# A two-layer vision tower on one core: moving preparation steps of the first attention to other chunks, and loading the second layer's weights and tokens during the expert attention

## The chip, the cores and the metric

The kernel runs on one core of a Trainium2 chip. The metric is the device time of one execution in microseconds (us); the time of a kernel is the median of its runs. A profile is one further execution, recorded by the hardware profiler, with an instruction-by-instruction trace.

## The reference

128 images of 128x128 pixels pass a convolutional tokenizer to 64 tokens of 256 features each. Two layers follow, each an attention and an "ffn", both with residual additions and a layer norm in front.

```
h = tokenizer(x)                                        # [128, 64, 256]
# layer 0
xn = layernorm(h); Q, K, V = xn @ Wq.T, xn @ Wk.T, xn @ Wv.T
attn[b,q,k,g] = relu(sum_d relu(Q[b,q,g,d] - K[b,k,g,d]) * w_mlp[d] + b_mlp)
h += softmax_k(attn) applied to V                       # 8 groups of 32 features
h = ffn0(layernorm(h))   # per 64-feature chunk: attention by 4 experts, gated, projected; plus residual
# layer 1
h += linear_attention(layernorm(h))  # softmax of q over features and of k over positions; k (x) v; times q
h += experts(layernorm(h))           # each token to one of 8 experts (capacity 1280), 256 -> 1024 -> 256
```

Everything is float32.

## The kernel before, in words

The stages run one after another: tokenizer; first attention (`relu_attention`); the ffn of layer 0 (`expert_attention`); the attention of layer 1 (`linear_attention`); routing and experts. Through the first three the activations stay on the chip in one tile `h2`, [128 partitions, 64 pairs of images, 256]; a partition holds one token of one of the two images of a pair. The order of the instructions is written out by hand: inside `tc.manual_schedule()` every engine executes its instructions in the order of the program.

**First attention.** Eight blocks of 16 images; each block is worked in eight chunks of eight query tokens, 64 chunks in all. A chunk needs, for 16 images and two halves of the features, the pairwise terms of queries and keys. They are made in three ways: `larger` (VectorE, a maximum, straight from the queries in PSUM), `difference` (GpSimd subtracts, ScalarE applies relu), and `by_query` (ScalarE alone, one token at a time). `add(i0, hf)` sums four images' terms over the features on TensorE. The eight additions of a chunk come in the order (0,0), (8,0), (4,0), (8,1), (0,1), (4,1), (12,0), (12,1); the first number is the first image, the second the half. Between them stand `queries` of the next chunk, `begin`, and the softmax of the chunk before: `less_max` on VectorE, `exponents` on ScalarE, `sums` on VectorE, `weights` on GpSimd, `transpose` on TensorE. The relu outputs pass through rings of buffers: `mg` has five, `ma` and `mv` three.

All that prepares the next block or finishes the last one is hung into the chunks by a table: `at(n, place, step)` puts a step into chunk n at a place. The places in the order of the program are O, X, A, V1, Y, B, W, Z, V2 and C; roughly, X, Y and Z are for TensorE, A, B, C and O for ScalarE, V1 and V2 for VectorE, W for GpSimd. With n = 8b for block b, `values(i)` (four pairs of projections of V) and their copies `valued(i)` are in chunks n-2, n-1 and n; `factors` (GpSimd: 1/sqrt(var) and the offset of the layer norm) at n-17 and n-13; `added(i)` (VectorE: outcome added to `h2`) in chunks n+10 to n+12. A chunk's number within its block of eight, n modulo 8, is called its position, or simply chunk 0 to chunk 7. Towards the end the places also hold the first steps of the expert attention (`beside`).

**Expert attention.** 64 pairs of images, one per turn of the loop in `rest`; each turn has the scores and softmax of pair p, the transposes, mixing and output of pair p-1 and the queries and values of pair p+1. `output` adds the result to `h2`, and every fourth pair a transfer on SP's queue stores four pairs to `hd`, a tensor in HBM.

**Linear attention.** It takes tokens in groups: a group is four token positions of all 128 images, so partition = image. `Group.load` brings a group from `hd`; `statistics` (VectorE), `factors` (GpSimd), `normal` (ScalarE) and `transpose` (TensorE, copied by ScalarE) prepare it. Four "heads" stages of 16 steps each then issue `queries_keys(i)`, while the table of this stage hangs in the rest. Before the first step come the loads of the weights on ScalarE's queue, of four groups on SP's queue, and the constants and the small loads of `Routing`.

SBUF tiles come from pools; a pool that opens where another was waits for the last use of that memory.

Of the kernel before, what the change touches and what calls it, by code (L numbers as in the profile page):

```python
# [290 lines left out]
class Shared:  # L291
# [3 lines left out]
    def __init__(self, c, ctx):  # L295
        def pool(name, bufs, **k):
            return ctx.enter_context(c.tc.tile_pool(name=name, bufs=bufs, **k))

        self.np_, self.bp = pool("an", 2), pool("ab", 2)
        self.atp, self.ep, self.small = pool("aat", 1), pool("ae", 2), pool("as", 1)  # L300
        self.psq = pool("apq", 4, space=PSUM)
# [5 lines left out]
def relu_attention(c, sh, wqkv, wmlp, bmlp, beside):  # L307
# [10 lines left out]
    with (  # L318
# [313 lines left out]
        for b, x in enumerate(blocks):  # L632
            n = 8 * b

            if b + 1 < len(blocks):
# [6 lines left out]
                for i in range(4):  # L642
                    at(n + 10 + i // 2, "XY"[i % 2], of(x.back, i))
                    at(n + 10 + (i + 1) // 2, ("V2", "V1")[i % 2], of(x.added, i))
# [15 lines left out]
            else:  # L660
                for i in range(NP):
                    at(n - 21 + i if b > 2 else 1 + i // 4, "V2", of(x.statistics, i))
                at(n - 17 if b > 2 else 2, "W", of(x.factors, 0, 4))
                at(n - 13, "W", of(x.factors, 4, 8))
# [16 lines left out]
            at(n - 2, "X", of(x.values, 0))  # L681
            at(n - 2, "A", of(x.valued, 0))
            at(n - 2, "Y", x.key_sums)
            at(n - 1, "V1", x.correction)
            at(n - 1, "X", of(x.values, 1))
            at(n - 1, "A", of(x.valued, 1))
            at(n - 1, "Z", of(x.values, 2))
            at(n, "O", of(x.valued, 2))
            at(n, "Y", of(x.values, 3))
            at(n, "B", of(x.valued, 3))  # L690
# [74 lines left out]
def expert_attention(c, sh, hd, normw, wr, br, wqkv, wvT, wproj, bproj, wout):  # L765
# [227 lines left out]
    class Pair:  # L993
# [89 lines left out]
        def weights(self, x):  # L1083

            e, sm = self.e[x], self.sm[x]
            s2 = sm.rearrange("p (m e) -> p m e", e=2)
            nc.gpsimd.tensor_mul(s2, s2, bcast(self.blk.gate[:, self.n, x::2], 1, 8))  # L1087
            nc.gpsimd.tensor_mul(e, e, bcast(sm, 2, T))  # L1088
# [31 lines left out]
        def output(self):  # L1120
# [5 lines left out]
            if p % 4 == 3:  # L1126
                nc.sync.dma_start(
                    hd[2 * p - 6 : 2 * p + 2].rearrange("(n b) t f -> (b t) n f", b=2),
                    h2[:, p - 3 : p + 1],
                )  # L1130

# [82 lines left out]
    def first(cur, new, chunk, last):  # L1214
# [39 lines left out]
        last.added(3)  # L1254
        for k in range(NB):
            x.stream(k)
# [3 lines left out]
    def rest(chunk, last):  # L1260
        with (
# [6 lines left out]
            for p in range(NP):  # L1268
                new = Pair(p + 1, blocks[(p + 1) // NB]) if p + 1 < NP else None
                if p == 0:  # L1270
                    first(cur, new, chunk, last)
                    old, cur = cur, new
                    continue
                do((p, "ACT"))
# [12 lines left out]
                cur.exponents(0)  # L1287
                if new:
# [8 lines left out]
                cur.weights(1)  # L1297
                do((p, "POOL"))
                old.mixed()
                if new:  # L1300
                    for h in range(2):
                        new.values(h)
                        new.values_kept(h)
                old.output()
# [11 lines left out]
def linear_attention(c, hd, hx, out, k, wqk, bqk, wv, bv, wgb):  # L1316
# [7 lines left out]
    NG = 4  # L1324
    with (
        tc.tile_pool(name="lw", bufs=1) as wp,
# [7 lines left out]
        w = wp.tile([P, 2, 2 * D], F32, name="w")  # L1334
        nc.scalar.dma_start(w, wqk.rearrange("(c p) n -> p c n", p=P))
        wvs = wp.tile([P, 2, D], F32, name="wvs")
        nc.scalar.dma_start(wvs, wv.rearrange("(c p) n -> p c n", p=P))
        bs = wp.tile([P, 2 * D], F32, name="bs")
        nc.scalar.dma_start(bs, bqk.partition_broadcast(P))
        bvs = wp.tile([P, 32], F32, name="bvs")  # L1340
        nc.scalar.dma_start(bvs, bv)

        wgs = wp.tile([P, 4, 32], F32, name="wgs")
        nc.gpsimd.memset(wgs, 0.0)
        for j in range(2):
            r = slice(j * 64, j * 64 + 64)
            nc.scalar.dma_start(wgs[r, :, j * E : j * E + E], wgb.rearrange("(p f) e -> f p e", f=64))
        ones = wp.tile([P, P], F32, name="ones")
        nc.gpsimd.memset(ones, 1.0)

        share = wp.tile([P, P], F32, name="share")
        nc.gpsimd.memset(share, 0.0)
        for hh in range(2):
            nc.gpsimd.memset(share[hh * 64 : hh * 64 + 64, hh * 64 : hh * 64 + 64], 1.0 / 64)

        class Group:
# [5 lines left out]
            def load(self):  # L1362
                g = self.g
                self.x = gp.tile([P, NG, D], F32, tag="x", name="x", bufs=4)
                nc.sync.dma_start(self.x, hd[:, g * NG : g * NG + NG, :])

            def statistics(self, j):
                if j == 0:
                    self.mv = gp.tile([P, NG, 2], F32, tag="mv", name="mv", bufs=4)
                    self.rs = gp.tile([P, NG], F32, tag="rs", name="rs", bufs=4)  # L1370
                    self.nb = gp.tile([P, NG], F32, tag="nb", name="nb", bufs=4)
                st = gp.tile([P, 6], F32, tag="st", name="st")
# [3 lines left out]
            def factors(self):  # L1376
                mean, var = self.mv[:, :, 0], self.mv[:, :, 1]
                nc.gpsimd.tensor_scalar_add(self.rs, var, LN_EPS)
                nc.gpsimd.tensor_tensor(self.rs, self.rs, c.nhalf[:, 0:NG], ALU.pow)
                nc.gpsimd.tensor_mul(self.nb, mean, self.rs)  # L1380
                nc.gpsimd.tensor_sub(self.nb, c.zero[:, 0:NG], self.nb)
# [250 lines left out]
        for n, x in enumerate(heads[:3]):  # L1632
# [35 lines left out]
            for k in range(2):  # L1668
                at(m + 1, 4 + 4 * k, x.gates, k)
                at(m + 1, 5 + 4 * k, x.gates_added, k)  # L1670

# [13 lines left out]
        def last():  # L1685
# [55 lines left out]
            t = gp.tile([P, NG, D], F32, tag="x", name="dev", bufs=4)  # L1741
            routing.statistics(t, gp.tile([P, NG, D], F32, tag="x", name="var", bufs=4))
# [22 lines left out]
        with tc.manual_schedule():  # L1765
            for g in range(4):
                groups[g].load()
            for g in range(3):
                for i in range(NG):
                    groups[g].statistics(i)  # L1770
                groups[g].factors()
                if g == 0:
                    for i in range(NG):
                        groups[0].normal(i)
                    groups[0].transpose()
            groups[4].load()
            for n, x in enumerate(heads):
# [15 lines left out]
class Routing:  # L1793


    def __init__(self, c, gp, wg, bg):
# [5 lines left out]
        self.bgs = gp.tile([P, E], F32, name="bgs")  # L1802
        nc.sync.dma_start(self.bgs, bg.partition_broadcast(P))
        wgs = gp.tile([P, 2, E], F32, name="wgs")
        nc.sync.dma_start(wgs, wg.rearrange("(c p) e -> p c e", p=P))
        self.ones = gp.tile([P, P], F32, name="ones")
        nc.gpsimd.memset(self.ones, 1.0)
        self.wsum = gp.tile([P, E], F32, name="wsum")
        with c.tc.tile_pool(name="gw", bufs=1, space=PSUM) as gpp:
            pw = gpp.tile([P, E], F32, name="pw")  # L1810
            for fc in range(2):
                nc.tensor.matmul(pw, self.ones, wgs[:, fc, :], start=(fc == 0), stop=(fc == 1))
            nc.vector.tensor_copy(self.wsum, pw)
# [13 lines left out]
        self.before = gp.tile([P, P], F32, name="before")  # L1827
# [4 lines left out]
        self.one = gp.tile([P, T], F32, name="one")  # L1832
        nc.vector.memset(self.one, 1.0)
        self.c = c
        self.mean, self.rs = (gp.tile([P, T], F32, name=n) for n in ("mean", "rs"))
# [329 lines left out]
def vit_tower(ctx: ExitStack, tc: tile.TileContext, a, out):  # L2165
# [8 lines left out]
    with tc.tile_pool(name="stream", bufs=1) as sp:  # L2174
        c.h2 = sp.tile([P, B // 2, D], F32, name="h2")
        tokenizer(c, a["x"], a["w1"], a["bn1"], a["w2"], a["bn2"])
        with ExitStack() as rings:
            sh = Shared(c, rings)
# [80 lines left out]
```

## Time and profile before

| | us |
|---|---|
| median of 3 runs (2669.07 to 2671.12) | 2670.72 |
| profiled execution, its own time | 2667.24 |
| its span, first to last instruction | 2665.5 |
| TensorE busy (share of the span) | 2523.5 (95%) |
| VectorE busy | 2009.8 (75%) |
| ScalarE busy | 1621.5 (61%) |
| GpSimd busy | 1627.9 (61%) |
| granted TensorE clock, mean | 0.983 |

Times inside the profile are microseconds from the span's start. PE is TensorE, PEld its weight loads, DVE VectorE, ACT ScalarE, POOL GpSimd, SP the engine whose queue issues most transfers. A line of the timeline or of the groups gives the engine, the line of the kernel (L340), the operation, "out<-in" by the program's names and, after "[", the idle time before it with what ended it. `x24` means that 24 instructions are merged. The chain of waits gives start, length and the instruction or transfer that everything after it waited for. A matmul's busy time counts pipelined instructions, so a busy TensorE may still wait inside.

The first attention runs from about 185 to 1060 us, with the additions as its largest row (L340), the expert attention until 1863.7, the linear attention until about 2160, routing until 2250 and the experts to the end.

### The profile page before, as it was taken

What the parts mean: (1) busy time and instruction counts of PE and PEld (TensorE: products, weight loads), DVE (VectorE), ACT (ScalarE), POOL (GpSimd) and SP (SyncE); (2) the same over time, 40 slices, a digit from 0 to 9 for tenths busy, and PEclk for the clock granted to TensorE, in tenths of its full rate; (3) what the DMA queues carried; (4) which work ended last, traced back from release to release, by engine and by line L of the source; (5) the groups of instructions that cost most, each with busy time, mean ns of one, the idle gap of its engine ahead of it and who ended that gap; (6) DMA issues with size and microseconds to landing.
All of it is one profiled execution on the core that took longest, in us unless ns stands there. A gap on an engine that the chain in (4) does not pass through costs nothing.

```text
span 2665.5 us, 81705 instructions
## 1 busy us (share of the span) xinstructions
PE 2523.5 (95%) x35613; PEld 1729.0 (65%) x35613; DVE 2009.8 (75%) x2998; ACT 1621.5 (61%) x3421; POOL 1627.9 (61%) x1426
## 2 busy tenths in 40 slices
PE   8989999999999999899999999998899987999997
PEld 4554444444444444688888888887466565888886
DVE  5759999999999999778787878776467786444443
ACT  2228889898898988666666666665344533232332
POOL 3319999999899999565666665643233313444544
PEclk9999999999999999999999999999899998999998
DMA  3000000000000000000000000000434454555554
GB/s 112 33 13 1 2 1 2 1 2 2 1 2 1 2 13 2 3 20 11 12 19 12 11 20 12 19 12 17 121 73 110 95 127 151 190 183 200 190 186 134
DMA packets 138274, 141.19 MB, mean 53 GB/s; under 512 B 107875, under 2 KB 121701, under 8 KB 130224
## 3 DMA queue, kind: packets, MB, share of 16 engines
q1 hardware_dynamic: 127536, 118.40, 14.7%
q0 software_dynamic: 7648, 14.77, 1.8%
q8 instruction: 281, 4.60, 0.7%
q10 hardware_dynamic: 2720, 2.69, 0.3%
q14 instruction: 89, 0.73, 0.1%
HBM read 104.03 MB, written 32.54 MB: 51 GB/s over the span
## 4 chain that ended last, share of the span: by engine, by line
PE 75%; DVE 13%; issue 5%; ACT 4%; POOL 2%; DMA 1%; SPq 0%; POOLq 0%; DVEq 0%; ACTq 0%
PE sc L340 15%; PE po L2103 6%; PE ph L2087 6%; PE pc L184 5%; PE pt L1097 4%; PE sc L1061 4%; PE pqk L1014 4%; PE pq L1421 4%; PE pv L1036 3%; PE pz L1110 3%; PE pt L587 2%; DVE m L530 2%; PE pc L459 2%; PE pk L405 2%; DVE mx L1073 2%
## 5 line engine op out<-in xcount | busy, mean ns | idle before, releaser
L538 POOL TENSOR_TENSOR m<-q,k 128x1024 f32<-128x1024 f32 x384 | 719.7, 1907 | 56.4 <-PE sc L340 44.5
L530 DVE TENSOR_TENSOR m<-pc,k 128x2048 f32<-128x2048 f32 (+1 forms) x320 | 646.4, 2056 | 0.5 <-ACT q L470 0.5
L340 PE MATMUL sc<-m,wide 128*32 128x512 f32 x4096 | 517.1, 597 | 8.5 <-ACT m L539 6.2
L539 ACT ACTIVATE m<-m 128x1024 f32<-128x1024 f32 x384 | 403.1, 1051 | 21.3 <-POOL m L538 21.3
L340 PEld LDWEIGHTS sc<-m,wide 128*32 128x32 f32 x4096 | 130.9, 109 | 270.1 <-issue 159.4
L548 ACT ACTIVATE m<-k,q 128x64 f32<-128x64 f32 x1024 | 271.1, 340 | 0.9 <-DVE k L417 0.9
L1073 DVE TENSOR_REDUCE mx<-sc 128x16 f32<-128x1024 f32 x128 | 156.0, 1219 | 135.3 <-PE sc L1061 135.3
L1088 POOL TENSOR_TENSOR e<-e,mx 128x1024 f32<-128x1024 f32 x128 | 243.5, 1902 | 10.1 <-POOL mx L1087 0.2
L1020 ACT COPY kr<-pqk 128x512 f32<-128x512 f32 x254 | 137.9, 604 | 142.1 <-PE pqk L1014 142.1
L2087 PE MATMUL ph<-xt,w1s 128*128 128x256 f32 x896 | 198.7, 379 | 3.4 <-DVE xt L2078 2.7
L1087 POOL TENSOR_TENSOR mx<-mx,gate 128x16 f32<-128x16 f32 x128 | 27.6, 216 | 280.3 <-ACT z L1118 150.9
L2103 PE MATMUL po<-w2s,hT 128*128 128x256 f32 x896 | 198.0, 379 | 0.0
L2087 PEld LDWEIGHTS ph<-xt,w1s 128*128 128x128 f32 x896 | 169.9, 190 | 27.9 <-DVE xt L2078 3.4
L2103 PEld LDWEIGHTS po<-w2s,hT 128*128 128x128 f32 x896 | 168.1, 190 | 21.7
L1100 ACT COPY pT<-pt 128x512 f32<-128x512 f32 x256 | 139.0, 600 | 51.6 <-PE pt L1097 51.4
L1074 DVE TENSOR_TENSOR e<-sc,mx 128x1024 f32<-128x1024 f32 x128 | 156.7, 1224 | 4.4
L2121 POOL DMA_INDIRECT out<-y,rout x56 | 56.7, 1013 | 167.8 <-ACT hT L2091 124.8
L1080 DVE TENSOR_REDUCE mx<-e 128x16 f32<-128x1024 f32 x128 | 152.5, 1191 | 4.6 <-ACT e L1077 4.5
L1097 PE MATMUL pt<-ident,e 128*128 128x128 f32 x1024 | 143.0, 282 | 10.0 <-DVE vr L1050 7.3
L2091 ACT ACTIVATE hT<-ph,w1s 128x256 f32<-128x256 f32 x224 | 93.0, 470 | 96.9 <-PE ph L2087 96.9
L2108 ACT ACTIVATE y<-y,gf 128x256 f32<-128x256 f32 x56 | 28.0, 507 | 196.0 <-issue 107.3
L1077 ACT ACTIVATE e<-e 128x1024 f32<-128x1024 f32 x128 | 139.6, 1090 | 1.6 <-DVE e L1074 1.6
(331 smaller groups left out, 5009.6 us busy)
## 6 DMA issues: line engine op xcount, KB each, us to landing
w1s<-in_we SPq DMA_DIRECT2D x30, 1028.0 KB, 5.1
w2s<-in_we SPq DMA_DIRECT2D x30, 1024.0 KB, 4.8
hd<-h SPq DMA_DIRECT2D x16, 512.0 KB, 3.2
x<-hd SPq DMA_DIRECT2D x16, 512.0 KB, 3.6
h<-hd SPq DMA_DIRECT2D x4, 2048.0 KB, 12.7
hx<-h SPq DMA_DIRECT2D x4, 2048.0 KB, 11.7
out<-h SPq DMA_DIRECT2D x4, 2048.0 KB, 20.5
xt<-in_x SPq DMA_DIRECT2D x15, 512.0 KB, 3.5
```

The lines of the kernel that those rows point to most:

```text
L340: nc.tensor.matmul(dst[j : j + 32], wide[:, hf, s : s + 32], part, start=start, stop=stop)
L530: nc.vector.tensor_tensor(m, bcast(self.pq[:, hf, i : i + n], 3, T), k, ALU.max)
L538: nc.gpsimd.tensor_tensor(m, bcast(self.q[:, hf, s : s + 2], 3, T), k, ALU.subtract)
L539: nc.scalar.activation(m, m, AF.Relu)
L548: nc.scalar.activation(self.parts[i, hf][:, q], self.blk.k[:, hf, i], AF.Relu, bias=self.q[:, hf, i - NB // 2, q : q + 1], scale=-1.0,)
L1073: nc.vector.tensor_reduce(mx, sc, AX.X, ALU.max)
L1074: nc.vector.tensor_sub(e, sc, bcast(mx, 2, T))
L1080: nc.vector.tensor_reduce(self.sm[x], self.e[x], AX.X, ALU.add)
L1088: nc.gpsimd.tensor_mul(e, e, bcast(sm, 2, T))
L1097: nc.tensor.transpose(pt[:, cq, :], e[:, i : i + 2, :].rearrange("p e s -> p (e s)"), c.ident)
L2087: nc.tensor.matmul(ph[:, j], self.w1[:, w0 : w0 + P], self.xt[:, fc], start=(fc == 0), stop=(fc == 1))
L2103: nc.tensor.matmul(po, self.hT[:, f, r * P : r * P + P], self.w2[:, f, :], start=(f == 0), stop=(f == 7))
```

## The change

In the first attention, three kinds of steps get other chunks: `values` (with `valued`), `factors` of the layer norm, and `added`. The words that name the change also speak of queries chunk by chunk.

Between the layers, a new class `Front` holds the weights, constants and the first four groups of tokens of the linear attention, in memory on the right side that two pools of the first attention (`aat`, `ae`) give back at the end of `first`. Weights are loaded at pair 8 of the expert attention. The tokens' rows follow the stores: after the store of four pairs, the rows of the eight images stored four pairs earlier are read back from `hd`; the last two images' rows are copied from `h2` without HBM. The last stores are of two, one and one pair. In the last turn, mixing and output of pair 62 stand earlier, three matmuls without use follow (`busy`), and the second half of the last weights is on VectorE. The linear attention begins with seven such matmuls, and its first group is normalized two rows at a time. The constants and small loads of `Routing` move into the first steps of the first head.

```diff
-        self.np_, self.bp = pool("an", 2), pool("ab", 2)
-        self.atp, self.ep, self.small = pool("aat", 1), pool("ae", 2), pool("as", 1)
+        self.np_, self.bp, self.small = pool("an", 2), pool("ab", 2), pool("as", 1)
+        self.atp, self.ep = (pool(n, k, end, side="right") for n, k in (("aat", 1), ("ae", 2)))
+        self.end = end
...
                 for i in range(4):
                     at(n + 10 + i // 2, "XY"[i % 2], of(x.back, i))
-                    at(n + 10 + (i + 1) // 2, ("V2", "V1")[i % 2], of(x.added, i))
+                    at(n + 10 + i // 2, ("V1", "V2")[i % 2], of(x.added, i))
...
-                at(n - 17 if b > 2 else 2, "W", of(x.factors, 0, 4))
-                at(n - 13, "W", of(x.factors, 4, 8))
+                at(n - 15 if b > 2 else 2, "W", of(x.factors, 0, 4))
+                at(n - 10, "W", of(x.factors, 4, 8))
...
-            at(n - 2, "X", of(x.values, 0))
-            at(n - 2, "A", of(x.valued, 0))
             at(n - 2, "Y", x.key_sums)
             at(n - 1, "V1", x.correction)
-            at(n - 1, "X", of(x.values, 1))
-            at(n - 1, "A", of(x.valued, 1))
-            at(n - 1, "Z", of(x.values, 2))
-            at(n, "O", of(x.valued, 2))
-            at(n, "Y", of(x.values, 3))
-            at(n, "B", of(x.valued, 3))
+            for i, (k, place) in enumerate(((6 - (b == 1), "Y"), (4, "Y"), (2, "X"), (1, "X"))):
+                at(n - k, place, of(x.values, i))
+                at(n - k, "BA"[place == "X"], of(x.valued, i))
...
             nc.vector.tensor_add(h2[:, p], h2[:, p], po)
-            if p % 4 == 3:
+            if p == NP - 1:
+                front.rows(B - 2, B)
+            n = {NP - 3: 2, NP - 2: 1, NP - 1: 1}.get(p, 4 * (p % 4 == 3))
+            if n:
                 nc.sync.dma_start(
-                    hd[2 * p - 6 : 2 * p + 2].rearrange("(n b) t f -> (b t) n f", b=2),
-                    h2[:, p - 3 : p + 1],
+                    hd[2 * (p - n + 1) : 2 * p + 2].rearrange("(n b) t f -> (b t) n f", b=2),
+                    h2[:, p - n + 1 : p + 1],
                 )
+            if p == NP - 3:
+                front.rows(B - 16, B - 8)
+            elif p == NP - 2:
+                front.rows(B - 8, B - 2)
+            elif n == 4 and p > 3:
+                front.rows(2 * p - 14, 2 * p - 6)
...
         last.added(3)
+        sh.end.close()
+        front.open()
...
+                if p == 8:
+                    front.weights()
...
                 cur.exponents(0)
+                if not new:
+                    old.mixed()
+                    old.output()
+                    c.busy(ps([P, 2 * D], "idle"), wt.w, 3)
...
-                cur.weights(1)
+                cur.weights(1, nc.gpsimd if new else nc.vector)
...
+    def rows(self, b0, b1):
+        nc, NG = self.c.nc, self.NG
+        n = 4 * NG
+        x = self.x.rearrange("p g t f -> p (g t) f")
+        if b1 < B:
+            nc.sync.dma_start(x[b0:b1], self.hd[b0:b1, 0:n, :])
+            return
+        for b in range(2):
+            nc.sync.dma_start(x[b0 + b : b0 + b + 1], self.c.h2[b * T : b * T + n, B // 2 - 1, :])
...
         with tc.manual_schedule():
+            c.busy(psp.tile([P, 2 * D], F32, tag="pp", name="idle"), w[:, 0], 7)
             for g in range(4):
-                groups[g].load()
+                groups[g].x = front.group(g)
             for g in range(3):
                 for i in range(NG):
                     groups[g].statistics(i)
-                groups[g].factors()
+                    if g == 0 and i % 2:
+                        groups[0].factors(i - 1, i + 1)
+                        for j in range(i - 1, i + 1):
+                            groups[0].normal(j)
                 if g == 0:
-                    for i in range(NG):
-                        groups[0].normal(i)
                     groups[0].transpose()
+                else:
+                    groups[g].factors()
             groups[4].load()
+            routing.load()
...
+        at(0, 9, routing.constants)
+        at(0, 10, lambda: routing.weights_sum(psp.tile([P, 2 * D], F32, tag="pp", name="pw")[:, 0:E]))
```

`Front.weights` issues, on SP's queue, the five weight and bias loads that stood on ScalarE's queue at the head of `linear_attention` (the gate weights in two halves), and the five memsets of its constants on GpSimd; `Routing.load` and `Routing.constants` are what stood in `Routing.__init__`.

## The prediction

> **What bounds the kernel now.** I read the stages first (busy time of each engine by stretch of the span), then the eight chunks of one block of the first attention, then the timelines of single engines in them, and last the chain of waits between the expert attention and the second layer. The stages: first attention 195 to 1100 us, expert attention to 1863.7, a hole, and the second layer's attention from 1882.4.
>
> ```profile
> 195.00:1100.00 905.00, 892.10 (x10595) 409.63 (x10597) 850.71 (x840) 797.82 (x1799) 820.30 (x534) 1.00 0.01 3
> 1100.00:1863.70 763.70, 734.27 (x19700) 648.23 (x19684) 603.04 (x871) 487.19 (x879) 451.76 (x505) 1.00 0.05 14
> 1863.70:1882.40 18.70, 3.61 (x13) 2.45 (x13) 6.83 (x29) 2.66 (x5) 6.42 (x23) 0.58 0.58 199
> ```
>
> The columns are the stretch, its length, the busy time of TensorE, of its weight loads, of VectorE, ScalarE and GpSimd, the granted clock, the DMA share and GB/s. TensorE fills both attentions and does 3.61 us of work in the 18.70 us of the hole. The chain there:
>
> ```profile
> 1863.30 0.43 DVE h L1125
> ...
> 1863.75 2.90 DMA hd<-h
> ...
> 1867.71 7.00 DMA x<-hd
> ...
> 1879.08 0.61 ACT x L1384
> ```
>
> The last addition, a store (2.90 us) on which everything waits, two small loads on SP's queue, and the tokens (7.00 us) beside all the weights. Then four rows of statistics, factors on GpSimd, four normalizations and eight transposes: from 1874.73 to the first query matmul at 1882.36, 7.6 us.
>
> One block of the first attention is eight chunks, here 523.99 to 634.05:
>
> ```profile
> 523.99:538.26 14.27, 14.27 (x134) 7.29 (x133) 12.73 (x14) 12.28 (x30) 13.68 (x11) 1.00 0.00 1
> 551.47:564.60 13.13, 12.90 (x243) 5.43 (x242) 12.72 (x13) 12.04 (x29) 12.25 (x8) 1.00 0.01 2
> sum 110.06, PE 109.83 PEld 49.84 DVE 104.20 ACT 98.87 POOL 101.32; mean PE 13.73 PEld 6.23 DVE 13.03 ACT 12.36 POOL 12.66
> ```
>
> TensorE looks full, but its timeline shows waits inside. An undisturbed run of 24 sum matmuls (three additions) takes 2.78 us; chunk 2 breaks one up, chunk 3 stretches one:
>
> ```profile
> 539.57 2.78 PE L340 MATMUL sc<-m,wide 128*32 128x512 f32 x24
> ...
> 561.24 1.05 PE L340 MATMUL sc<-m,wide 128*32 128x512 f32 x4
> 562.52 1.91 PE L340 MATMUL sc<-m,wide 128*32 128x512 f32 x12 [0.23 <-ACT m L539]
> ...
> 578.48 3.75 PE L340 MATMUL sc<-m,wide 128*32 128x512 f32 x24
> ```
>
> Adding up undisturbed pieces of each chunk (one addition 0.87, `queries` 1.0, `values` 1.82, keys 1.91, outcome 1.42 and so on) against its length (start to start in TensorE's timeline) gives these waits per block: chunk 2 1.8 us, chunk 3 1.3, chunk 4 1.1, the others 0 to 0.2. 105.5 us of 110.06 are work.
>
> **What holds a chunk.** Let T be the start of a chunk's first addition (533.34 in this chunk 0). VectorE's maximum of the chunk before can only start at T; after it come, in order, a 2.2 us maximum, the sums, and the maximum for addition (4,1):
>
> ```profile
> 533.61 0.70 DVE L564 TENSOR_REDUCE pc<-sc 128x8 f32<-128x512 f32 x1 [1.33 <-PE sc L340]
> ...
> 535.23 2.28 DVE L530 TENSOR_TENSOR m<-pc,k 128x2048 f32<-128x2048 f32 x1
> ...
> 538.26 3.37 DVE L530 TENSOR_TENSOR m<-pc,k 128x2048 f32<-128x2048 f32 x2
> ```
>
> The first of the last pair is done at about 540.5, T+7.16; `added` at place V1 makes that T+7.75. ScalarE's last relu for addition (8,1) likewise ends at 539.31, T+5.97 (T+6.16 where a normalization at C precedes). These two floors recur in other chunks. A chunk with too little TensorE work before those additions waits.
>
> **What the skill says.** "TensorE: Matmul & The Clock Gate", section "What's actually happening": the clock halves after about 3.4 us of idleness. The trace agrees: 0.58 granted in the hole. "DMA: Bandwidth & Descriptors", "Two DMAs through the same engine are not ordered": a load of rows just stored must wait for the store's completion; here POOL and SP wait for hd (2.90 us). "SBUF — State Buffer", "Who interferes with whom": VectorE with two SBUF inputs contends with GpSimd's reads. The trace has no case at this place, so I allow it up to 1.9 us, GpSimd's own multiply, and take 0.2.
>
> **The change, part by part.** (a) *Values.* One `values` (1.82 plus a 0.59 copy on ScalarE) leaves chunk 0 and one leaves chunk 7; chunks 2 and 4 each get one. The total stays. Chunk 7: 14.3 to 12.5; its additions still meet the floors, since its X step (1.92) stays. Chunk 0: the addition (8,1) would start at T+4.4, but its relus end at T+6.16, so (4,1) starts near T+7.5 instead of T+6.1: the chunk falls from 13.2 to about 12.7, not 11.4. Chunk 2: its wait at (8,0) comes before Y and stays, 0.5 of later waits is covered: +1.3. Chunk 4: +1.8, and 0.7 of waits goes: +1.1.
> (b) *Additions.* `added(3)` leaves V1 of chunk 4 (counted above); `added(0)` comes to V1 of chunk 2, where the new `values` covers its 0.6. Chunk 3 keeps one at V1 and its wait: 0.
> (c) *Factors.* Four GpSimd operations, 2.0 us in the queue, move from chunks 3 and 7 to 1 and 6. Behind them stands the difference (14,0), and its relu and addition (12,0). In chunk 1 that relu ended at T+10.42; it moves to T+11.2 against a use at T+11.40: 0. In chunk 6 it moves to T+11.2 against T+11.04: a wait and a split of an addition, +0.4. Chunk 3 gains 0.1.
> Block: -0.5 -1.8 +1.3 +1.1 +0.4 -0.1 = **+0.4 us**; over the blocks with first and last chunks +2.7 us. Both ends: the waits of chunks 2 to 4 all vanish (-2.5 a block, -17), or chunks 0 and 7 keep their lengths and 2 and 4 grow in full (+3.6 a block, +25).
> (d) *"Queries chunk by chunk"*: no line of the diff touches the first attention's `queries`, which already take eight tokens a chunk: 0.
> (e) *Weights and tokens early.* Four loads and two small ones at pair 8 and eighteen row loads stand on SP's queue, where only the hd stores pass (SP's longest wait there is 42 us, for the addition before a store), so they cost nothing. Five memsets of 0.2 us on GpSimd at pair 8 lie in its idle time before the weights' first multiply (280.3 us in 128 times, 2.2 each). The only late rows are of the last pair: two copies within SBUF, after the last addition. Such a copy is not in the trace: small loads landed in 1.7 us (4 KB, wr) to 3.9 us (bgs, contended); I take 0.4 issue plus 2.3. Then two rows of statistics 1.2, factors 1.6 and, for the second pair, 1.6 more (a 128x2 power is 0.72 against 1.04), two normalizations 1.2, transposes and copy 1.0: 6.7. From the addition to the first query matmul 9.4 instead of 18.6: **-9.2** (-7.5 to -10.5). The seven idle matmuls (6.0 us) keep the clock, which was half until 1883.9: -0.6.
> (f) *Last pair.* `output` of pair 62 goes ahead of the sums on VectorE and delays them 1.4 us, so the first weights end at 1856.4 instead of 1854.9; the second, on VectorE (1.22), end then too instead of at 1857.1; transposes run at full clock (1.09 against 1.97): -0.4, from -1.2 to +0.8. Three idle matmuls lie in waiting time.
> (g) *Routing's constants* leave the hole: 1.9 us of GpSimd beside other work, four small matmuls and a PSUM turn in head 0, where TensorE is the bound: +0.6 (0 to 1.2). Its two loads follow group 4's on SP and are needed ten steps later.
>
> **Sum:** 2.7 - 9.2 - 0.6 - 0.4 + 0.6 = -6.9 us. The profiled execution took 2667.24 us (span 2665.5 and 1.7 around it), so 2660.3; the median of the runs is 3.5 above it: 2663.8, say **2664**.
>
> **Rivals.** *The rearrangement pays:* the balance removes most waits of chunks 2 to 4, -2 a block; for it speaks that each moved step has a wait beside it, against it the floors, which follow T. 2664 - 17 = 2647; chance 0.12. *The rearrangement costs:* chunks 0 and 7, emptied, fall back on ScalarE's and VectorE's floors, and what chunks 2 and 4 take on is not given back. Place: additions (8,1) and (4,1) of chunk 0. From 2.1 us a block on it passes the gain of the hole: at 2.5, 17.5 - 9.6 = +8, 2679; at the bound 2686. For it speaks chunk 60, with little beside, which still takes 13.5; against it chunk 6 at 12.8 without waits. Chance 0.12. *The hole barely shrinks:* the last copies land as late as the 7 us load, or readers of the one big x tile wait for the next group's load: -5 instead of -9.2, near 2668.5; chance 0.16. My own case has 0.60, spread over 2658 to 2670.
>
> **Numbers.** A measurement of this kernel tells about 0.2% (5.3 us) from no change. My case lies mostly beyond it at 2665.4 (0.46 of its 0.60 faster, 0.14 same); the first rival faster, the third same but for a little. Faster 0.58, same 0.29, slower 0.13. Range 2655 to 2674.
>
> **What would show it.** First query matmul 9 to 10 us after the last addition; clock near 1 there; chunk 7 at 12.5, chunk 0 at 12.7 with a wait at (8,1), chunk 4 at 16.4, blocks of 110 to 111 us. A block under 109 or over 112, or a hole over 13 us, proves me wrong.

## The result, and the profile after

The changed kernel takes 2661.46 us (median of 13 runs, 2654.66 to 2666.34) where the kernel before, run beside it, takes 2669.07 (13 runs, 2664.71 to 2671.85): a ratio of **0.9974** (95% interval 0.9965 to 0.9983), 7.6 us between the medians. The prediction had 2664.0 and a sum of -6.9 us.

The profiled execution of the changed kernel happens to be its fastest run (2654.66 us, span 2652.9, mean clock 0.989), so its trace is 12.7 us shorter than the trace of before, not 7.6. The experiment called `e_rows` below turned out to execute the same instructions in the same order on every queue, and its profiled execution (span 2658.0) serves as a second trace of the change. Both against before, by stage, in us:

| stage | after | second trace |
|---|---|---|
| start to TensorE's last addition of the first attention | +2.35 | +2.29 |
| to VectorE's last addition to `h2` in the expert attention | -2.75 | -0.36 |
| to the first query matmul of the second layer | **-9.02** | **-9.02** |
| to the second head | -0.30 | -0.30 |
| to the end | -2.94 | -0.1 |
| sum | -12.66 | -7.5 |

The third row is the same in both traces and is what the change does. Of the first row, 0.48 and 0.35 us lie ahead of the first addition, where the change moves nothing; from the first addition to the last (200.2 to 1080.1 us in before) it is +1.87 and +1.94, and this is the price of the new table. The second and the last row differ between two executions of one order of work, and come back below.

The stages of after (stretch, length, busy time of PE, PEld, DVE, ACT, POOL, granted clock, DMA share, GB/s):

```profile
195.00:1100.00 905.00, 891.82 (x10499) 412.13 (x10498) 850.21 (x840) 798.41 (x1799) 818.76 (x532) 1.00 0.01 3
...
1863.30:1872.90 9.60, 8.03 (x22) 3.52 (x22) 6.17 (x26) 2.79 (x6) 4.35 (x13) 1.00 0.06 18
```

The hole is 9.6 us instead of 18.7, at full clock. TensorE's 8.03 us in it are mostly idle matmuls. Its timeline (all engines, most rows left out; start, duration, engine and line):

```profile
1862.90 0.42 DVE L1122 TENSOR_TENSOR h<-h,po 128x256 f32<-128x256 f32 x1 [5.36 <-PE po L1121]
1863.35 1.25 SPq L1385 DMA_DIRECT2D x<-h  x2
...
1866.34 0.43 DVE L1425 BATCH_NORM_STATS2 st<-x 128x6 f32<-128x256 f32 x1 [3.02 <-DMA x<-h]
...
1869.23 1.09 ACT L1437 ACTIVATE x<-x,nb,rs 128x256 f32<-128x256 f32 x2 [7.55 <-POOL nb L1434]
...
1872.93 1.55 PE L1474 MATMUL pq<-w,xT 128*128 128x512 f32 x3 [0.24 <-ACT xT L1447]
```

Read downwards: the last addition ends at 1863.32; the two copies within SBUF let VectorE start 3.02 us later; from there to the first query matmul it is 6.6 us (statistics, factors, two pairs of normalizations, transposes).

One steady block, cut where TensorE starts a chunk's first addition: chunks 0, 2, 4 and 7 of eight.

```profile
533.67:547.27 13.60, 13.31 (x125) 5.39 (x120) 13.39 (x13) 12.45 (x30) 13.36 (x9) 1.00 0.01 1
...
560.40:575.31 14.91, 14.69 (x136) 6.77 (x132) 14.00 (x15) 13.89 (x33) 13.44 (x9) 1.00 0.01 2
...
588.39:604.25 15.86, 15.86 (x132) 6.73 (x128) 13.96 (x13) 13.75 (x34) 12.25 (x8) 1.00 0.00 1
...
631.34:643.93 12.59, 12.59 (x124) 6.20 (x120) 12.36 (x14) 11.97 (x28) 12.59 (x8) 1.00 0.01 2
sum 110.26, PE 109.75 PEld 50.27 DVE 104.18 ACT 99.24 POOL 101.23; mean PE 13.72 PEld 6.28 DVE 13.02 ACT 12.40 POOL 12.65
```

Before, the same four chunks, cut in the same way:

```profile
533.34:546.55 13.21, 13.21 (x133) 6.21 (x128) 12.72 (x12) 11.97 (x28) 12.30 (x8) 1.00 0.01 1
...
559.69:573.35 13.66, 13.44 (x129) 5.74 (x125) 13.25 (x14) 13.30 (x32) 12.26 (x8) 1.00 0.01 2
...
586.53:601.79 15.26, 15.26 (x127) 5.59 (x122) 14.46 (x14) 14.35 (x35) 13.97 (x9) 1.00 0.00 1
...
628.89:643.41 14.52, 14.52 (x134) 7.27 (x130) 13.25 (x14) 13.29 (x33) 13.86 (x12) 1.00 0.01 2
sum 110.07, PE 109.84 PEld 49.85 DVE 104.20 ACT 98.89 POOL 101.33; mean PE 13.73 PEld 6.23 DVE 13.03 ACT 12.36 POOL 12.67
```

Chunk 7 gave up 1.93 us; chunks 2 and 4 took 1.25 and 0.6; chunk 0, from which 1.82 us of work was removed, became 0.39 *longer*.

### The profile page after: what moved, and what is told of

It reads as the page before. It is cut to its first block, busy times and chain, and to the rows that moved or that the text cites. A ratio compares the mean times of both kernels' runs of the same rounds, so it can differ in the third digit from the quotient of the medians.

```text
span 2652.9 us, 81755 instructions
## 1 busy us (share of the span) xinstructions
PE 2526.2 (95%) x35633; PEld 1730.8 (65%) x35633; DVE 2012.2 (76%) x3000; ACT 1623.1 (61%) x3421; POOL 1625.8 (61%) x1428
```

## The experiments

My theory after these traces: the whole gain is the hole, and the new table of the first attention is worth nothing. Rivals: the table pays or costs several us; the hole's gain comes from the clock and not from the transfers. A third question appeared in the first traces: what the early loads cost inside the expert attention.

### The table alone, and the front alone

`e_table`: before, with the three edits of the table. `e_front`: the changed kernel, with the table of before. The edits are shortened here.

```diff
 e_table, to the kernel before
-  at(n + 10 + (i + 1) // 2, ("V2", "V1")[i % 2], of(x.added, i))
+  at(n + 10 + i // 2, ("V1", "V2")[i % 2], of(x.added, i))
-  at(n - 17 ...factors 0, 4)   at(n - 13 ...factors 4, 8)
+  at(n - 15 ...factors 0, 4)   at(n - 10 ...factors 4, 8)
-  values at n-2 X, n-1 X, n-1 Z, n Y
+  values at n-6 Y, n-4 Y, n-2 X, n-1 X
 e_front: the same lines the other way round, in the changed kernel
```

> The kernel before with the changed table of the first attention alone (values, factors, additions). Theory (the floors): a steady block takes 110.27 us instead of 110.06, chunk 0 13.6, chunk 7 12.6; the first attention ends 2.3 us later and the whole takes 2 to 3 us longer than before, ratio 1.0009. Rival (the rearrangement pays, and the hole gave less than it seems): a ratio under 0.999.

> The changed kernel with the first attention's table of before, so the early loads and the last turn alone. Theory: from the last addition to the first query matmul 9.6 us as in the changed kernel, blocks of 110.06 us, about 9.5 us less than before, ratio 0.9965. Rival (the rearrangement pays): not better than the changed kernel's ratio of 0.9974.

Measured: `e_table` 2669.06 us, ratio 0.9998 (0.9990 to 1.0006); its block takes 110.27, chunk 0 13.60 and chunk 7 12.60, as in after; from the first addition to the last it is 1.96 us longer than before. I had expected 1.0009; the interval ends at 1.0006, so the times do not show even the two us of the trace. `e_front` 2659.56 us (5 runs), ratio 0.9954 (0.9941 to 0.9967), the hole shorter by 9.03, the block 110.04. What follows: the hole carries the gain; the table costs two us in the trace, and in the times no cost can be seen.

### Additions and factors alone

`e_addfac`: before, with the edits of `added` and `factors` only.

> The kernel before, with the new places of the additions and of the factors, and the old places of the value projections. Theory (moving these costs nothing, the values alone change the block): chunk 4 loses the addition at V1 and with it some of its waits, 15.26 to about 14.9; chunk 2 gets one, 13.66 to at most 13.9; chunk 6 keeps 12.78 though the factors now stand in its W, chunk 3 13.1; the block 109.8 to 110.1. My prediction instead had the factors cost chunk 6 0.4 us: it would show 13.2 there, and a wait of TensorE at the addition (12,0).

Chunks 3 and 6:

```profile
576.31:589.76 13.45, 13.22 (x128) 5.59 (x124) 13.24 (x15) 12.34 (x30) 12.25 (x8) 1.00 0.01 1
...
619.37:632.15 12.78, 12.78 (x161) 6.81 (x156) 12.29 (x12) 10.57 (x23) 12.37 (x11) 1.00 0.00 1
```

Chunk 6 keeps its 12.78 with the factors in it: they cost nothing, and my 0.4 was wrong. But the block is 110.37, over the 109.8 to 110.1 expected: chunk 3 is longer by 0.27 (its addition (8,1) waits 0.38 more) and chunk 4, though it lost an addition on VectorE, takes 15.29 and is not shorter: a wait of 0.42 at (0,0) is gone, and others at (8,1) and (4,1) came in its place. Additions and factors moved together here, and chunk 3 has as many additions as before, so which of the two costs chunk 3 its 0.27 was not separated. In the changed kernel a value projection in chunk 4 fills just that time: 15.87 - 15.29 = 0.58 for 1.82 us of work. The time, 2673.20 us, is of a single execution, and is no evidence either way.

### Where value projections cost least

`e_keep0`, `e_2x` and `e_7z` are the changed kernel with other places for the four projections.

```diff
-  enumerate(((6 - (b == 1), "Y"), (4, "Y"), (2, "X"), (1, "X")))
+  enumerate(((5, "Y"), (2, "X"), (1, "X"), (0, "Y")))              # e_keep0: chunks 3, 6, 7, 0
+  enumerate(((6 - (b == 1), "X"), (5, "Y"), (2, "X"), (1, "X")))   # e_2x: chunks 2, 3, 6, 7
+  enumerate(((6 - (b == 1), "X"), (5, "Y"), (2, "X"), (1, "Z")))   # e_7z: its copy in the next O
```

> The changed kernel with the four values at other chunks: the last stays in chunk 0 at Y, the first goes to chunk 3 at Y, two stay at X of chunks 6 and 7. Theory (a chunk without work before addition (8,1) waits for the floors, so work put there is nearly free): chunk 0 13.2 instead of 13.6, chunk 3 13.7 instead of 13.1, chunk 2 13.7 instead of 14.9, chunk 4 14.6 instead of 15.9; a block 108.3 to 109.0 us; 15 to 18 us less than before, ratio 0.993 to 0.9945. Rival (TensorE's work alone sets a block, wherever it stands): blocks of 110 us and a ratio of 0.9965.

> The changed kernel, with the four value projections beside chunks 2 (place X), 3 (Y), 6 (X) and 7 (X) instead of 2 (Y), 4 (Y), 6 (X) and 7 (X). Theory (a projection costs nothing where TensorE would wait next, and its full 1.82 where nothing waits): in chunk 2 it now stands ahead of the addition (8,0), whose wait of 0.85, and the 0.42 after it, it covers, so chunk 2 takes 13.8 to 14.1 instead of 14.91; chunk 3 takes 13.84 as with the values there before, chunk 4 14.88, chunk 0 keeps 13.60; the block comes to 109.0, 1.3 under the changed kernel's 110.27, and the time to 0.9925 to 0.994 of before. Rival (the start of the chunk's later maxima moves with what stands at X, so that the waits only move): chunk 2 takes 15.0 to 15.5, the block 110.1 to 110.5 and the time is the changed kernel's 0.997.

> The changed kernel, with the value projections beside chunks 2 (place X), 3 (Y), 6 (X) and 7 (Z, its copy in chunk 0's O), so that chunk 7 loses its step at X and chunk 0 has none. The question is why chunk 0 takes 13.60 without a projection, and not the 12.7 of my prediction, which left chunk 7's end as it was. Theory A (the end of chunk 7 sets it: with a projection at Z the additions at chunk 7's end come later against the relus of ScalarE, and the wait of 0.38 and 0.42 at chunk 0's (8,0) and (4,0) is gone): chunk 0 takes 12.6 to 12.9. Theory B (an emptied chunk 0 has its floor at 13.6 by itself): 13.4 to 13.7. Chunk 7 waits at its (8,0) in both, 13.5 to 14.3, so the block gains nothing: 108.9 to 109.9, 0.9935 to 0.997 of before.

`e_keep0`: 2651.52 us (5 runs), ratio **0.9931** (0.9918 to 0.9944). Chunk 0 and the whole block:

```profile
529.80:543.80 14.00, 14.00 (x132) 6.37 (x128) 13.62 (x13) 13.03 (x31) 13.36 (x9) 1.00 0.01 1
...
529.80:639.00 109.20, 108.98 (x1273) 50.77 (x1269) 104.10 (x102) 99.23 (x225) 101.26 (x65) 1.00 0.01 2
```

`e_2x`: 2653.27 us (5 runs), ratio 0.9946 (0.9932 to 0.9960). Chunk 2 and the block:

```profile
556.02:570.16 14.14, 14.14 (x136) 7.07 (x132) 13.74 (x15) 13.79 (x33) 13.44 (x9) 1.00 0.01 2
...
529.28:638.20 108.92, 108.62 (x1273) 50.93 (x1269) 104.23 (x102) 99.15 (x225) 101.28 (x65) 1.00 0.01 2
```

The same 1.82 us of matmuls cost 1.25 in chunk 2 at Y, 0.48 there at X (13.66 to 14.14: it stands ahead of the addition (8,0), whose wait it covers), 0.77 in chunk 3 at Y, 0.40 in chunk 0 at Y. The block falls by 1.1 to 1.3 us against after; from the first addition to the last it is 5.3 us (`e_keep0`) and 6.6 us (`e_2x`) shorter than before. The theory of `e_2x` holds for the block and for chunks 0, 2 and 3, and its rival falls; chunk 4 took 14.51 where I expected 14.88, which nothing here explains, and the ratio is 0.0006 above the expected range. Of `e_keep0` the block stands 0.2 over the upper end I expected, for chunk 0.

`e_7z` asks about that chunk: 2659.27 us (5 runs), ratio 0.9964 (0.9950 to 0.9977), block 109.94, at the upper end of what I expected. It differs from `e_2x` in one thing only: the projection of chunk 7 stands at Z instead of X. Chunks 7 and 0:

```profile
629.92:644.15 14.23, 13.75 (x124) 6.04 (x120) 13.35 (x14) 13.41 (x33) 13.76 (x9) 1.00 0.01 2
534.21:547.20 12.99, 12.59 (x124) 5.23 (x120) 12.50 (x12) 11.01 (x25) 12.25 (x8) 1.00 0.00 1
```

With a projection at the end of chunk 7, chunk 0 without one takes 12.99, and not 13.60 as in after (13.61 in `e_2x`), and its wait of 0.8 us at (8,0) and (4,0) is gone: nearer to theory A, though 0.1 over what it gave. TensorE's timeline shows the rest. In after, where T = 533.67:

```profile
538.96 1.05 PE L342 MATMUL sc<-m,wide 128*32 128x512 f32 x4
540.30 2.34 PE L342 MATMUL sc<-m,wide 128*32 128x512 f32 x18 [0.29 <-ACT m L541]
542.38 0.60 PE L525 MATMUL sc<-kb,ident 128*32 128x512 f32 x2
542.47 0.60 PE L342 MATMUL sc<-m,wide 128*32 128x512 f32 x2
```

and in `e_7z`, where T = 534.21:

```profile
538.81 1.05 PE L342 MATMUL sc<-m,wide 128*32 128x512 f32 x4
540.24 2.34 PE L342 MATMUL sc<-m,wide 128*32 128x512 f32 x18 [0.37 <-ACT m L541]
```

The second half of the addition (8,1) starts at T+6.63 in after and at T+6.03 in `e_7z`. The floor of T+6.16 in my prediction holds where chunk 7's end is as it was; it is not counted from T alone.

### What makes the hole short

`e_viahd`: the changed kernel, the last two images' rows read from `hd` behind their store. `e_nobusy`: without the three and the seven idle matmuls. The edit of `e_viahd` is shortened; `rows` also loses its branch for the copies.

```diff
 e_viahd
-  if p == NP - 1:  front.rows(B - 2, B)          # copies from h2, ahead of the store
...
+  elif p == NP - 1:  front.rows(B - 2, B)        # loads from hd, behind it
 e_nobusy
-  c.busy(ps([P, 2 * D], "idle"), wt.w, 3)
-  c.busy(psp.tile([P, 2 * D], F32, tag="pp", name="idle"), w[:, 0], 7)
```

> The changed kernel, with the rows of the last two images read from hd after their store instead of copied within SBUF ahead of it. Theory (the copy is what makes the hole short, since a load from hd must wait for the store): store 2.1 to 2.9 us and a load of 1.9 to 2.5 instead of a copy of 3.0 to landing, so the first query matmul 11 to 12 us after the last addition instead of 9.6, the time 1.5 to 2.5 us above the changed kernel's. Rival (the two memory paths overlap or the rest of the chain sets the start): 9.6 to 10.2.

> The changed kernel without its ten matmuls that compute nothing (three in the last turn, seven ahead of the linear attention). Theory: the hole stays at 9.6 us within 0.5, because no waiting work is behind them, but the clock is at half in the first queries: 0.5 to 2 us longer than the changed kernel, ratio to before 0.9976 to 0.998. Rival (the clock carries much of the gain): 3 us or more longer, ratio over 0.9985.

`e_viahd`, a single execution: 2662.85 us. In its timeline:

```profile
1867.85 0.42 DVE L1122 TENSOR_TENSOR h<-h,po 128x256 f32<-128x256 f32 x1 [5.36 <-PE po L1121]
...
1870.01 0.24 SPq L1380 DMA_DIRECT2D x<-hd  x1
...
1872.62 0.43 DVE L1420 BATCH_NORM_STATS2 st<-x 128x6 f32<-128x256 f32 x1 [4.35 <-DMA x<-hd]
```

The load goes out 1.7 us after the small store (issued at 1868.30) and the statistics start 4.35 us after the addition's end, where the copy let them start 3.02 after it; the first query matmul comes 11.0 us after the last addition instead of 9.6. So the copy is worth 1.4 of the 9.0 us. The rest, that only two images are left to the end and that their factors go two rows at a time, was not taken apart by a run.

`e_nobusy`: 2665.29 us (8 runs), ratio 0.9976 (0.9965 to 0.9986), which is the changed kernel's. The hole is nearly as short (-8.88), so its gain does not come from the clock. In its trace the clock is half from 1874.3 to 1884.5, and the first head takes 1.55 us longer than in after. The idle matmuls do keep the clock up on the whole: its mean is 0.983 to 0.985 in the eight runs without them, and 0.985 to 0.989 in every run of a kernel that has them. But the 1.55 us are no proof of a gain in time: of the ten traces that have them, five also lose 0.9 to 1.4 us against before in the first head (`e_front`, `e_2x`, `e_viahd`, `e_skip15`, `e_7z`), to a half-clock slice of 3.4 us in or near it, and five gain 0.30. "TensorE: Matmul & The Clock Gate", section "What's actually happening", of the Trainium skill says that the activity window is free-running and its phase varies from run to run; two groups of values, with nothing between, fit that. What ten idle matmuls are worth in time stays open.

### The last weights on VectorE

`e_pool`: the changed kernel with `cur.weights(1)` for every pair, so on GpSimd.

> The changed kernel, with the weights of the last pair's second image on GpSimd again instead of on VectorE. My prediction says that VectorE ends them 0.7 us earlier (at the first weights' end instead of 1.9 us behind them less what they start earlier). Rival, from the trace of the changed kernel: VectorE's multiply only starts when GpSimd's ends, and its small one takes 0.90 instead of 0.2 meanwhile, so that VectorE saves only the difference of 1.90 and 1.22: the last addition 0.4 to 0.9 us later than in the changed kernel. If the two would run beside each other, more than 1.2.

In after, GpSimd's first multiply and VectorE's two instructions:

```profile
1854.35 1.90 POOL L1085 TENSOR_TENSOR e<-e,mx 128x1024 f32<-128x1024 f32 x1
...
1855.38 0.90 DVE L1084 TENSOR_TENSOR mx<-mx,gate 128x16 f32<-128x16 f32 x1
1856.32 1.22 DVE L1085 TENSOR_TENSOR e<-e,mx 128x1024 f32<-128x1024 f32 x1
```

The small multiply takes VectorE 0.90 (GpSimd takes 0.21 for its own of this shape) and ends with GpSimd's; then the large one runs. This is the case that I had not found before: "SBUF — State Buffer" of the Trainium skill, section "Who interferes with whom", calls the ports that the two engines share an exclusive lock, and the trace agrees to 0.03 us (GpSimd ends at 1856.25, the small multiply at 1856.28). In `e_pool` the second weights end 4.1 us after the first start (1861.18 to 1865.23), in after 3.2 us (1854.35 to 1857.54): VectorE saves 0.9, the upper end of the rival. Counted from the first weights, the last addition comes 1.9 us later in `e_pool`; the other 1.0 goes with a half-clock slice there (1865.8 to 1869.2), which after does not have. The time of this single execution is 2663.51 us.

### The early loads and the instruction fetch

In eight of the nine traces of kernels that load rows behind the store of pair 15, pair 17 of the expert attention takes 14.2 to 17.1 us; in after it takes 12.35, and in before, `e_table` and `e_addfac`, which have no early loads, 12.19. `e_front` shows what happens (TensorE's timeline):

```profile
1296.20 0.37 PE L1016 MATMUL pqk<-xTr 64*128 64x128 f32 x1
1299.39 1.28 PE L1016 MATMUL pqk<-xTr 64*128 64x128 f32 x15 [2.82 <-issue]
1300.60 3.48 PE L1112 MATMUL pz<-pT,vr 128*64 128x64 f32 x64
```

TensorE stands 2.82 us with nothing to wait for, and then runs at half clock (3.48 us for what normally takes 2.09). In the trace's transfers an instruction fetch (16 KB) starts 2.3 us after the pair in before, in `e_front` 3.9 us, just where the store of 512 KB and the row load of 128 KB behind it end, and takes 1.6 instead of 0.9 us. In all fourteen traces TensorE goes on 1.4 to 1.6 us after the end of this fetch, whenever that is. After has the same transfers, but its fetch started at 2.6 us, where the store ended, ahead of the row load, which ran until 4.65: TensorE stood 0.96 us. So it depends on which of the two comes first, and the profiled execution of after was the one trace in nine with the good order.

First try, `e_rows`: each row load two pairs later in the program.

```diff
-  elif n == 4 and p > 3:
-      front.rows(2 * p - 14, 2 * p - 6)
+  elif p == 59:
+      front.rows(B - 24, B - 16)
+  elif p % 4 == 1 and p > 8:
+      front.rows(2 * p - 18, 2 * p - 10)
```

> The changed kernel, with each row load of 128 KB two pairs later than the hd store instead of straight behind it. Seen so far: in three profiles of kernels with the early loads, TensorE stands 2.82 us on issue in pairs 17 to 18 of the expert attention and then runs at half clock, where an instruction fetch queues behind a store of 512 KB and the row load. Theory A (the row loads, put straight behind the stores, delay instruction fetches): no such wait in the profile, the pairs all near 12.1 us, and a median 2 to 4 us under the changed kernel's 0.9974 of before, so 0.996. Theory B (the wait comes from the store alone or from elsewhere): the wait of 2.8 us shows again and the time is the changed kernel's, 0.997 to 0.998. The loads themselves cost nothing in either.

It says nothing on this: 2661.30 us (12 runs), ratio 0.9970 (0.9961 to 0.9979), pair 17 at 15.76; and SP's timeline shows why:

```profile
1291.83 0.38 SPq L1128 DMA_DIRECT2D hd<-h  x1
1292.31 0.33 SPq L1384 DMA_DIRECT2D x<-hd  x1
```

On SP's queue nothing lies between a store and the next load in the program, so the load leaves straight behind the store wherever it is written. The second try removes one load:

```diff
-  elif n == 4 and p > 3:
-      front.rows(2 * p - 14, 2 * p - 6)
+  elif n == 4 and p > 3 and p != 15:
+      front.rows(2 * p - 14 - 8 * (p == 19), 2 * p - 6)
```

> The changed kernel, without the row load of 128 KB behind the hd store of pair 15; its eight rows come with the next load. (Putting the loads two pairs later in the program had not moved them on SP's queue: nothing there holds them back after the store ahead.) Theory A (the row load occupies a DMA engine on which the instruction fetch of pair 17 stands, and TensorE runs out of instructions): the fetch starts 2.3 us after the start of pair 17 instead of 3.9, TensorE's wait of 2.82 us and the half clock behind it are gone, the pair takes 12.2 instead of 15.7, and the time is 2 to 3.5 us less, 0.996 of before. Theory B (the wait comes from the store or another source): the pair takes 15.7 again and the time is the changed kernel's 0.997.

> The changed kernel, with the value projections beside chunks 2 (X), 3 (Y), 6 (X) and 7 (X) and without the row load at pair 15. Theory: the two gains add, block 108.9 and pair 17 at 12.2, the time 0.992 to 0.994 of before. Rival: another fetch meets a load, and the time stays at 0.9946, that of the new places alone.

TensorE in `e_skip15`, the same three rows and, later, pair 21:

```profile
1297.05 0.37 PE L1011 MATMUL pqk<-xTr 64*128 64x128 f32 x1
1298.03 1.16 PE L1011 MATMUL pqk<-xTr 64*128 64x128 f32 x15 [0.61 <-issue]
1299.12 2.08 PE L1107 MATMUL pz<-pT,vr 128*64 128x64 f32 x64
...
1348.75 2.58 PE L1107 MATMUL pz<-pT,vr 128*64 128x64 f32 x61 [1.83 <-issue]
```

Without the load the fetch starts at 2.2 us, the wait is 0.61 (in before 0.63), and pair 17 takes 12.19: theory A is right at this place, and `e_best` shows it too (12.20). But the time is 2662.03 us (14 runs), ratio 0.9978 (0.9970 to 0.9986), no better than the changed kernel and not the 0.996 expected: pair 21, which the doubled load now precedes, takes 14.89 against 12.20. There the fetch starts 4.3 us after the pair, where that load ends, so removing one collision made another. `e_best`, with the places of `e_2x` as well, takes 2651.60 us (5 runs, 2650.82 to 2653.20), ratio **0.9938** (0.9924 to 0.9951), block 108.90, as expected; that is not to be told from `e_2x` or `e_keep0`. Its pair 21 takes 13.04, with a wait of 1.55 us behind the same load and no half clock. All three beat both kernels, and how the loads would have to be spread to cost nothing stays open.

## Why the prediction was right, and where it wasn't

**The hole (e), right.** -9.2 predicted, -9.02 in both traces. Its terms: copy to landing 2.7, measured 3.0; rows to query matmul 6.7 (the pieces named there add up to 6.6), measured 6.6. The rival of a hole that barely shrinks is out.

**The table (a to c), right in sum and wrong in its largest part.** Block +0.4, measured +0.20; first attention +2.7, measured +1.9 from the first addition to the last. By chunk: 7 at -1.8 (measured -1.93), 2 at +1.3 (+1.25), 4 at +1.1 (+0.61), 6 at +0.4 (0), 0 at **-0.5 (+0.39)**. The step that failed is "the addition (8,1) would start at T+4.4, but its relus end at T+6.16": I held the floors of chunk 0 for fixed to its own start, while the same edit took the projection out of chunk 7's end, which lets T come sooner than the relus behind it. `e_7z` puts that at 0.6 us; 0.3 more comes in the addition (4,1), which is broken up there and takes 0.42 longer than in the chunk 0 of before; I had no term for that. Chunk 4 failed the other way: of its 1.8 us I let 0.7 go into waits, and 1.2 did. Errors of +0.9, -0.5 and -0.4 cancelled, which is luck.

**Additions (b)** at 0 held in the sum only: with the factors, and without the values, chunk 3 is 0.27 longer. **Factors in chunk 6 (c)** at +0.4: nothing; the addition (12,0), whose relu stands behind them, waits no longer than before.

**Queries (d)** at 0: nothing in the trace contradicts it; `queries` take the same 1.0 to 1.1 us in each chunk.

**"They cost nothing" (e), wrong.** I looked at SP's queue for what the loads would delay and found nothing; the instruction fetch, which has no line in the program, was not on my list. In eight of nine traces it cost 2 to 5 us at pair 17 (2.0 in the two that kept their clock there, 3.5 and more in the six with half clock). "Runtime: NRT & Kernel Launch" of the Trainium skill, section "Instruction fetch mechanics", says that blocks of 16 KiB are fetched ahead by the sequencer's own queue and that this is mostly hidden; the size is that of the trace, the hiding fails here behind 640 KB of other transfers, and the 0.63 us of before show that it was not complete without them. What it does to the median isn't settled: `e_skip15` gained nothing.

**The last pair (f)** -0.4, measured -0.53 (18.99 to 18.46 us from the start of pair 63 to the last addition), but that is luck. I let the second weights end with the first, and they end 1.3 behind them (1856.25 and 1857.54). The transposes at full clock (1.09) were as I had them, but the traces point to the clock and not to the new order: before has 6.8 us of half clock in its last turn, and `e_table` and `e_addfac`, with the old order and 3.4 us of it, take 18.13. Eight traces of the new order with none there take 18.2 to 18.7. That the new order gains anything is not shown.

**The clock (-0.6) and routing's constants (+0.6)** can't be parted: together -0.30 in the first head of both traces, but +0.9 to +1.4 in five of the ten traces with the idle matmuls. What I had no step for are the stages behind: -2.9 us in after, about 0 in the second trace, from -3.2 to +2.3 in the others. That a sum of -6.9 met 7.6 us is in part luck: pair 17 and these stages can each outweigh all that I had beside the hole. The largest part of the -2.9 in after is the last head, which has two half-clock slices less; first before, then after:

```profile
2070.52:2137.45 66.93, 60.65 (x434) 36.31 (x433) 48.77 (x80) 33.99 (x67) 23.84 (x16) 0.92 0.40 83
```

```profile
2059.79:2124.47 64.68, 57.96 (x434) 35.09 (x433) 48.75 (x80) 34.08 (x67) 22.27 (x16) 0.97 0.40 86
```

The stage with the same 434 matmuls takes 2.25 us less at a clock of 0.97 against 0.92; in `e_7z`, with the same code there as in after, the last head takes 67.21. This goes with the phase of the slices: in all fourteen traces one begins 28.35 to 29.21 us into the last head; where it begins at 28.61 or earlier (nine traces, before among them), one or two more follow, and where it begins at 28.87 or later (five, after among them), none does. Whether the change shifts this phase, or chance does, is not shown.

**The rivals.** "The rearrangement pays" is false for these places (0.9998 for the table alone) but its mechanism is real: with the projections elsewhere the block falls to 108.9, 6.6 us in all. "The rearrangement costs" had named the right place, chunk 0, and too high a price; its break-even is 1.4 us a block (9.6 over seven blocks), not 2.1.

## What to carry to other kernels

Between two stages, count what must wait for the very last result: everything else can be loaded before, and the last piece moved by the shortest way there is. A moved step costs what TensorE had to do there beyond its next wait, from 0.4 to 1.25 us for one and the same 1.82; and a chunk's floor depends on what stands at the end of the chunk before it. A transfer that "hides" in an idle queue could still hold up an instruction fetch, as here in eight traces of nine: look for waits on issue near each large one. And before a difference of 1 to 2 us is put down to a change, compare the granted clock in that stage in both traces.

## What the runs showed of the hardware that was not expected

- An instruction fetch of 16 KB that has to wait behind a 512 KB store and a 128 KB load starts 1.6 us later and takes 1.6 us instead of 0.9 (`e_front` against before); TensorE stands 2.82 us instead of 0.63, and the half clock after it adds 1.4.
- A VectorE multiply of 128x16 took 0.90 us beside a GpSimd multiply (GpSimd's own of this shape takes 0.21), and the next one began 0.07 us after GpSimd's end; in the ten traces with this order the gap is 0.06 or 0.07.
- A copy of two 16 KB rows within SBUF was usable 3.02 us after the addition it waited for; a store and a load through HBM of the same rows 4.35.
- Between executions of the same order of work, pairs of the expert attention vary by waits on issue (pair 20 took 12.80 us in before, 11.61 in after and 13.15 in the second trace of the same order); the stage differs by 2.4 us between the two traces of the change.
